# Cross-attention with prompt tokens: the bulk loads issued from GpSimd instead of SyncE

## The chip, the cores and the metric

The kernel runs on one core of a Trainium2 chip. A core has TensorE (PE) for matmuls, VectorE (DVE), ScalarE (ACT), GpSimd (POOL) and SyncE (SP), each with an instruction queue of its own that is worked off in order, and 16 DMA engines that move data between device memory and the on-chip memory. A transfer is started by an instruction in the queue of one of these engines; the engine that starts it need not be the one that uses the data. The metric is the device time of one execution, in microseconds (us). Before the change it is 423.75 us, the median of three runs from 422.22 to 429.26.

## What is computed

Eight batches of 112 rows of x (320 channels) attend to 375 context rows of 512 numbers each, in 20 heads of 16 channels. The last 4 context rows are prompt tokens with weights of their own. Cut to what matters:

```
q   = heads(x @ W_q)
k_t = heads(text @ W_k);  v_t = heads(text @ W_v)          # 371 rows
probs_t  = softmax(q k_t^T * scale)
text_out = probs_t v_t
k_ip = heads(ip @ W_k_ip); v_ip = heads(ip @ W_v_ip)       # 4 rows
qsem  = l2norm(probs_t text);  sem = qsem l2norm(ip)^T
probs_ip = softmax(q k_ip^T * scale + 0.5 * sem) * mask
out = (text_out + probs_ip v_ip) @ W_out + b_out + x
```

All in fp32.

## The kernel before, in words

**Tiling and order.** A batch is worked off in 5 groups of 4 heads (`steps`, line 1101: 40 pairs of batch and group). PE's four row groups of 32 take one head each. Heavy work of a group is `multiplied` (line 768): the transposed probabilities of 4 heads, in 12 blocks of 32 context rows, times a matrix `u`. `u` holds for each block of context rows the Gram matrix of the context (from which the length of qsem comes without qsem itself), the products with the prompt tokens, a column of ones, and 16 columns with the values of the head. The Gram part is made once for each batch (`gram`, line 516, `doubled`, line 502) and brought to all four row groups by DMAs (`gram_to_groups`, line 549). The 16 value columns differ from group to group: `placed` (line 681) copies them on POOL from `vr` into `u`, in three chunks of four blocks (the copies of line 688). A chunk's copy for the next group has to wait until PE has read that chunk for the present group, and PE cannot begin the chunk in the next group before the copy is done. `u` has two buffers, for even and odd batches.

**What comes before a group.** PE makes the scores (line 719), DVE their maximum (line 742), ACT the exponentials (line 745), a DMA of SP deals the probabilities out to the row groups (`sent`, line 754, tile xg), DVE transposes them (line 762). Between the groups stands the work for the next batches: context transposed (line 437), keys (line 577), values (line 611), Gram matrix (line 535), queries (lines 363 to 386, from x in blocks, tile xr_sb, which DVE transposes on line 365). After a batch `finish` (line 844) and `prompt_sums_and_projection` (line 968) work its output out; POOL multiplies the prompt values there (lines 970 to 978), and PE needs the result for line 983.

**Loads.** Context rows of batch 2 and later come by `load_ctx_blocks` (line 150): four DMAs of 352 rows of 512 bytes and four of 19 rows, after a memset of the last block on POOL (line 156), into tile ct, which has two buffers. x comes by `load_x_blocks` (four DMAs of 28 partitions, line 127, into the two places of xr_sb) and once more whole by `load_x` (line 1212, x_sb) for the residual. The prompts' values go to device memory (line 334) and come back once for each batch as `vip` (line 644) or, for the last two batches, by way of `vipx` and `bd` (lines 651 and 663). The second copy of W_q (rows in another order, lines 121 and 122), the prompts' weights (line 137, wkip_sb and wvip_sb), W_out (lines 133 and 134), mask and bias (lines 1217 and 1218) come while the first batch is under way. All of these are issued by SP, whose queue also carries xg, u (line 553), vd and vr (the values by way of device memory, lines 627 and 636) and the output. The first loads (lines 178 to 193: context of batches 0 and 1, W_v, x of batch 0, W_q, W_k) are SP's too.

**What sets the order.** The program is recorded by a framework that plans the order of each engine's queue. `tc.manual_schedule` keeps the written order: in the prologue (line 96, closed on line 1209) for all engines, for the main loop for PE, SP, DVE (line 93) and ACT (line 1245). POOL is among them only from line 1324 on, for the last batch. Elsewhere the planner places POOL's instructions, and may put one far ahead of where it is written if what it depends on is there and its buffer is free. For each queue that issues DMAs the framework has eight semaphores, used in turn: a DMA also waits until the one eight before it has landed.

```
    def placed(b, g, chunks=range(NT)):
        s = st[b]
        for c in chunks:
            v = region(b, c)[:, :, UV - c * P :]
            ...
            nc.gpsimd.tensor_copy(v, dealt(b, c, s["vr"][:, c * QN : (c + 1) * QN, g, :]))
...
    engines = {mybir.EngineType.PE, mybir.EngineType.SP, mybir.EngineType.DVE}
    ctx.enter_context(tc.manual_schedule(engines=engines))
```

Of the kernel before, what the change touches and what calls it, by code (L numbers as in the profile page):

```python
# [20 lines left out]
def kernel(  # L21
# [14 lines left out]
    nc = tc.nc  # L36
    P = 128
    B, S, C = x.shape
# [46 lines left out]
    def bank(name, spare=False):  # L85
# [13 lines left out]
    x_sb = const.tile([S, B, C], F32, tag="x_sb", name="x_sb")  # L99

    xr_sb = const.tile([P, 2, QN, C // QN + 4], F32, tag="xr_sb", name="xr_sb")
    wq_sb = const.tile([P, NC, CP], F32, tag="wq_sb", name="wq_sb")
# [4 lines left out]
    wkip_sb, wvip_sb = (  # L107
        work.tile([P, NIP, H, D], F32, tag="vipb", name=name).rearrange("p e h d -> p e (h d)")
        for name in ("wkip_sb", "wvip_sb")
    )  # L110
    wo_sb = const.tile([P, NC, C], F32, tag="wo_sb", name="wo_sb")
    ip_sb = const.tile([N, E], F32, tag="ip_sb", name="ip_sb")
    sm_sb = const.tile([S, 1], F32, tag="sm_sb", name="sm_sb")
    bias_sb = const.tile([S, C], F32, tag="bias_sb", name="bias_sb")
# [3 lines left out]
    def load_pairs(eng, t, w):  # L118

        w = w.rearrange("(p c) f -> p c f", c=5)  # L120
        eng.dma_start(t[0::2, :, :C], w[:, :3, :])
        eng.dma_start(t[1::2, :2, :C], w[:, 3:, :])

    def load_x_blocks(b, j):

        for a in range(QN):
            nc.sync.dma_start(
                xr_sb[a * RG : a * RG + S // QN, j, :, :XB],
                x[b, :, a * XB : (a + 1) * XB].rearrange("(q i) f -> i q f", q=QN),
            )  # L130

    def load_channels(eng, t, w):
        eng.dma_start(t[:, :FULL, :C], w[: FULL * P, :].rearrange("(i p) f -> p i f", p=P))
        eng.dma_start(t[:REST, FULL, :C], w[FULL * P :, :])

    def load_embed(eng, t, w):
        eng.dma_start(t[:, :, :C], w.rearrange("(p e) f -> p e f", e=NE))
# [12 lines left out]
    def load_ctx_blocks(b, blocks=range(QN)):  # L150

        full = TT // RG
        if b not in loaded:
            ct = io.tile([P, NT, E], F32, tag="ct", name=f"ct_{b}")
            v = ct.rearrange("p c e -> p (c e)").rearrange("p (j f) -> p j f", f=P)
            nc.gpsimd.memset(v[:, full, :], 0.0)
            loaded[b] = v
        v = loaded[b]
        for a in blocks:
            nc.sync.dma_start(  # L160
                v[a * RG : (a + 1) * RG, :full, :],
                ehs[b, : full * RG, a * P : (a + 1) * P].rearrange("(j i) f -> i j f", i=RG),
            )
        for a in blocks:
            nc.sync.dma_start(
                v[a * RG : a * RG + TT - full * RG, full, :],
                ehs[b, full * RG : TT, a * P : (a + 1) * P],
            )

    def load_ctx(b):  # L170
        if b >= LEAD:
            load_ctx_blocks(b)
            return loaded[b]
        ct = io.tile([P, NT, E], F32, tag="ct", name=f"ct_{b}")
        for c in range(NT):
            rows = min(P, T - c * P)
            some = rows - rows % 16
            nc.sync.dma_start(ct[:some, c, :], ehs[b, c * P : c * P + some, :])
            if some < rows:
                nc.sync.dma_start(ct[some:rows, c, :], ehs[b, c * P + some : c * P + rows, :])  # L180
        return ct
# [71 lines left out]
    vipx = dram.tile([2, H, NIP, C], F32, tag="vipx", name="vipx", bufs=1)  # L253
# [387 lines left out]
    def prompt_values(b):  # L641

        st[b]["vip"] = work.tile([P, NIP, H, D], F32, tag="vipb", name=f"vip_{b}")[:S]
        nc.sync.dma_start(
            st[b]["vip"].rearrange("p n h d -> p (n h d)"),
            vipd[b * NIP : (b + 1) * NIP, :].rearrange("n c -> (n c)").partition_broadcast(S),
        )

    def prompt_values_by_head():

        nc.sync.dma_start(
            vipx,
            vipd[N - 2 * NIP :, :]
            .rearrange("(b n) c -> b n c", n=NIP)
            .unsqueeze(1)
            .to_broadcast([2, H, NIP, C]),
        )

    def load_prompt_values_by_head():
        t = io.tile([P, NT, E], F32, tag="ct", name="bd")  # L660
        st[B - 1]["xb"] = t[:S, 2, :C]
        bd = t[:HN, :2, :CP]
        nc.sync.dma_start(bd[:, :, :C], vipx.rearrange("b h n c -> (h n) b c"))
        return bd

    def own_channels(bd):
# [14 lines left out]
# [5 lines that stand above are left out]
            if b > 0 and c > 0:  # L686
                v = v.rearrange("p (i j) d -> p i j d", i=2)
            nc.gpsimd.tensor_copy(v, dealt(b, c, s["vr"][:, c * QN : (c + 1) * QN, g, :]))  # L688
# [49 lines left out]
    def probabilities(b, g, a, hold=False):  # L738
        s = st[b]
        ps = s.pop(("sc", g, a))  # L740
        nmx = small.tile([S, 1], F32, tag="nmx", name=f"nmx_{b}_{g}_{a}", bufs=4)
        nc.vector.tensor_reduce(nmx, ps[:S, :TT], AX.X, ALU.max, negate=True)  # L742
        if ("p", g) not in s:
            s["p", g] = home(b, g)
        nc.scalar.activation(s["p", g][:, a, :], ps[:S, :TT], AF.Exp, bias=nmx)  # L745
        if b > 0:
            nc.scalar.copy(s["ipl"][:, groups[g][a], :], ps[:S, TT:T])  # L747
        if not hold:
            sent(b, g, a)
# [442 lines left out]
    drain(transposed_context(1))  # L1192
    run(("q", 0), None)
    nc.gpsimd.memset(wq_sb[:, FULL, :], 0.0)
    load_pairs(nc.sync, wq_sb, w_q)
    load_x_blocks(1, 0)
    run(("k", 0), None)
    for a in range(GROUP):
        scores(0, 1, a, early=True)
        probabilities(0, 1, a)  # L1200
    load_embed(nc.sync, wkip_sb, w_k_ip)
    load_embed(nc.sync, wvip_sb, w_v_ip)
    placed(0, 0)
    transposed(0, 0)
    run(("k", 0), None)
# [3 lines left out]
    prologue.close()  # L1209

    def load_x(b0, b1):
        nc.sync.dma_start(x_sb[:, b0:b1, :], x[b0:b1].rearrange("b s c -> s b c"))

    def load_rest(n):

        if n == 3:
            nc.sync.dma_start(sm_sb, smask.unsqueeze(1))
            nc.sync.dma_start(bias_sb, b_out.partition_broadcast(S))
        elif n == NG + 1:
            load_channels(nc.sync, wo_sb, w_out)  # L1220
        if g == NG - 1:
            load_x(b, b + 1 if b < B - 2 else B)

# [22 lines left out]
    for n, (b, g) in enumerate(steps[:-NG]):  # L1246
# [5 lines left out]
        for j, _ in enumerate(multiplied(b, g)):  # L1252
            if j == 0:
                for c, a in now if late else ():
                    scores(*c, a)
                    probabilities(*c, a)
                for c, a in more:
                    scores(*c, a, ps=bank(f"ps_s_{c[0]}_{c[1]}_{a}"))
                    probabilities(*c, a, hold=True)
            if j == 6:  # L1260
                for c, a in then:
                    scores(*c, a)
            if j == 2:
                if g == 0:
                    gram_banks(b + 1)
                transposed(*steps[n + 1])
                for c, a in more:
                    sent(*c, a)
                if 1 <= g <= 3:
                    gram_to_groups(b + 1, {1: (0,), 2: (1,), 3: (3,)}[g], parts=halves[g == 2])  # L1270
                for c, i in x_loads.get((b, g), ())[: int(n > 0)]:
                    load_x_blocks(c, i)

                if g in (1, 2) and b > 0:
                    run(("f", b - 1), None)
# [14 lines left out]
        if g == 0 and b > 1:  # L1290
            run(("f", b - 2), None)
        load_rest(n)
        if n == 0:
            load_next(2)
        if g in ctx_blocks and b < B - 3:
            load_ctx_blocks(b + 3, ctx_blocks[g])
        for c, i in x_loads.get((b, g), ())[1:]:
            load_x_blocks(c, i)
# [10 lines left out]
        if (b, g) == (B - 2, 0):  # L1309
            prompt_values_by_head()  # L1310
        if (b, g) == (B - 2, 1):
            bd = load_prompt_values_by_head()
        if g == 0 and b > 0:
            prompt_values(b - 1)
# [15 lines left out]
    b = B - 1  # L1330
# [6 lines left out]
    for g in range(NG):  # L1337
# [28 lines left out]
        n = (3, 3, 2, 1)[g]  # L1366
# [90 lines left out]
```

## Time and profile before

| | us |
|---|---|
| median of three runs | 423.75 |
| the profiled execution | 426.04 |
| its span, first to last instruction | 424.3 |
| PE busy | 415.8 |
| DVE busy | 331.5 |
| ACT busy | 185.5 |
| POOL busy | 111.2 |

The profile is of one execution. Busy time is the time in which an engine has an instruction under way; PE's matmuls are pipelined and their ends are modelled, so a busy PE is not PE at its peak. Issues of DMAs and waits are not counted as busy. A row of a timeline has the start, the time taken, engine, line, operation, output and input with shapes, a count, and in brackets the idle time before it and what ended that. A row of the busy times by stage has the stretch, its length, the busy time of PE, PE's weight loads, DVE, ACT and POOL with their instruction counts, the clock granted to TensorE (1.00 is full), the share of the DMA engines and GB/s. Over the span the granted clock is 0.999, and the DMA engines move 155 GB/s on the mean, nearly all of it from SP's queue.

### The profile page before, as it was taken

What the parts mean: (1) busy time and instruction counts of PE and PEld (TensorE: products, weight loads), DVE (VectorE), ACT (ScalarE), POOL (GpSimd) and SP (SyncE); (2) the same over time, 40 slices, a digit from 0 to 9 for tenths busy, and PEclk for the clock granted to TensorE, in tenths of its full rate; (3) what the DMA queues carried; (4) which work ended last, traced back from release to release, by engine and by line L of the source; (5) the groups of instructions that cost most, each with busy time, mean ns of one, the idle gap of its engine ahead of it and who ended that gap; (6) DMA issues with size and microseconds to landing.
All of it is one profiled execution on the core that took longest, in us unless ns stands there. A gap on an engine that the chain in (4) does not pass through costs nothing.

```text
span 424.3 us, 14021 instructions
## 1 busy us (share of the span) xinstructions
PE 415.8 (98%) x5500; PEld 327.3 (77%) x5500; DVE 331.5 (78%) x693; ACT 185.5 (44%) x647; POOL 111.2 (26%) x277
## 2 busy tenths in 40 slices
PE   8999999999998999999999999999999999999995
PEld 8867767878776977779778887788778887787993
DVE  5037668869896987889789987987898986888873
ACT  2344332335333463334533463333634363446773
POOL 6411100011160120602133220602124120515550
PEclk9999999999999999999999999999999999999999
DMA  8676846565766565666656556655555556465200
GB/s 256 184 191 198 187 122 181 155 174 152 192 157 169 141 170 154 158 175 175 169 142 167 144 158 164 159 145 158 167 151 151 134 162 181 135 167 166 66 2 29
DMA packets 61687, 65.84 MB, mean 155 GB/s; under 512 B 22072, under 2 KB 55648, under 8 KB 61622
## 3 DMA queue, kind: packets, MB, share of 16 engines
q1 hardware_dynamic: 60990, 63.98, 56.5%
q8 instruction: 44, 0.72, 0.8%
q10 hardware_dynamic: 632, 0.96, 0.7%
q14 instruction: 21, 0.17, 0.1%
HBM read 20.23 MB, written 5.32 MB: 60 GB/s over the span
## 4 chain that ended last, share of the span: by engine, by line
PE 83%; DVE 4%; ACT 3%; DMA 3%; issue 3%; SPq 2%; POOL 0%; DVEq 0%; POOLq 0%
PE ps_qd L781 34%; PE ps_v L611 14%; PE ps_k L577 10%; PE ps_s L719 9%; PE ps_g L535 7%; DMA xg<-p 2%; PE ps_q L377 2%; PE ps_o L995 2%; PE ps_g L491 1%; DVE xgT L762 1%; DVE nmx L742 1%; ACT shared L820 1%; SPq L553 1%; PE ps_w L467 1%; SPq L636 1%
## 5 line engine op out<-in xcount | busy, mean ns | idle before, releaser
L781 PE MATMUL ps_qd<-u,xgT 32*112 32x360 f32 (+11 forms) x3840 | 219.5, 351 | 1.2 <-POOL u L688 1.2
L781 PEld LDWEIGHTS ps_qd<-u,xgT 32*112 32x112 f32 x3840 | 189.1, 172 | 27.0 <-POOL u L688 2.4
L762 DVE STREAM_TRANSPOSE xgT<-xg 128x1536 f32<-128x1536 f32 (+1 forms) x45 | 119.7, 2680 | 13.9 <-DMA xg<-p 9.4
L745 ACT ACTIVATE p<-ps_s,nmx 112x371 f32<-112x371 f32 x156 | 84.9, 586 | 61.5 <-DVE nmx L742 49.3
L742 DVE TENSOR_REDUCE nmx<-ps_s 112x1 f32<-112x371 f32 x160 | 76.9, 526 | 28.3 <-PE ps_s L719 27.3
L827 DVE CUSTOM_DVE_ANT_0 junk<-ps_qd,p 112x371 f32<-112x371 f32 x146 | 79.2, 543 | 17.9 <-PE ps_qd L781 1.5
L719 PE MATMUL ps_s<-kT,qm 32*112 32x375 f32 (+1 forms) x320 | 66.7, 497 | 0.0
L688 POOL COPY u<-vr 128x64 f32<-128x64 f32 x120 | 25.7, 236 | 152.5 <-PE ps_qd L781 90.2
L611 PE MATMUL ps_v<-wv_sb,ctxT 128*128 128x384 f32 (+1 forms) x192 | 63.0, 477 | 0.0
L611 PEld LDWEIGHTS ps_v<-wv_sb,ctxT 128*128 128x128 f32 x192 | 35.7, 190 | 20.9
L794 ACT COPY pvs<-ps_qd 112x21 f32<-112x21 f32 x151 | 16.2, 189 | 74.8 <-PE ps_qd L781 74.5
L577 PE MATMUL ps_k<-ctxT,wk_sb 128*128 128x371 f32 x136 | 46.9, 488 | 0.2 <-DVE ctxT L458 0.2
L577 PEld LDWEIGHTS ps_k<-ctxT,wk_sb 128*128 128x128 f32 x136 | 24.4, 189 | 14.0 <-issue 0.5
L719 PEld LDWEIGHTS ps_s<-kT,qm 32*112 32x112 f32 x320 | 23.7, 170 | 12.6 <-issue 10.9
L535 PE MATMUL ps_g<-ctxT 128*32 128x375 f32 (+11 forms) x672 | 30.4, 333 | 0.0
L535 PEld LDWEIGHTS ps_g<-ctxT 128*32 128x32 f32 x672 | 27.7, 110 | 2.0
L618 ACT COPY vext<-ps_v 128x384 f32<-128x384 f32 (+1 forms) x24 | 11.2, 465 | 40.0 <-PE ps_v L611 39.5
L747 ACT COPY ipl<-ps_s 112x4 f32<-112x4 f32 x140 | 24.3, 174 | 0.0
L386 DVE TENSOR_SCALAR qm<-ps_q,emask 128x224 f32<-128x224 f32 (+1 forms) x25 | 9.0, 394 | 17.3 <-PE ps_q L377 17.2
L970 POOL TENSOR_TENSOR wv<-vip,w 112x1280 f32<-112x1280 f32 x6 | 14.8, 2464 | 27.7 <-DVE w L910 27.7
L437 DVE STREAM_TRANSPOSE ctxT<-ct 128x512 f32<-128x512 f32 x18 | 20.0, 1110 | 0.0
L508 POOL TENSOR_TENSOR ug<-ug,half 128x128 f32<-128x128 f32 (+1 forms) x24 | 10.4, 447 | 30.6 <-ACT ug L507 30.6
(174 smaller groups left out, 320.7 us busy)
## 6 DMA issues: line engine op xcount, KB each, us to landing
xg<-p SPq DMA_DIRECT2D x156, 162.3 KB
u<-ug SPq DMA_DIRECT2D x124, 99.0 KB
ct<-in_ctx_dram SPq DMA_DIRECT2D x24, 176.0 KB
vr<-vd SPq DMA_DIRECT2D x32, 120.0 KB
vip<-vipd SPq DMA_DIRECT2D x6, 560.0 KB
vd<-vext SPq DMA_DIRECT2D x7, 320.0 KB
vd<-vext SPq DMA_DIRECT2D x7, 160.0 KB
out_dram<-ob SPq DMA_DIRECT2D x8, 140.0 KB
```

Source lines behind the costliest of these rows:

```text
L437: nc.vector.transpose(ctxT[:, :, c * P : (c + 1) * P].rearrange("p e (j i) -> p j e i", i=RG), ct[:, some, :].rearrange("p j (k e) -> p j ...
L535: nc.tensor.matmul(ps[c][q * RG : (q + 1) * RG, j * RG - c * P : T - c * P], ctxT[:, e, j * RG : (j + 1) * RG], ctxT[:, e, j * RG : T], st ...
L577: nc.tensor.matmul(ps[:, :TT], wk_sb[:, e, i * P : (i + 1) * P], s["ctxT"][:, e, :TT], start=(e == 0), stop=(e == NE - 1),)
L611: nc.tensor.matmul(ps[:, :w], ctxT[:, e, c * P : (c + 1) * P], wv_sb[:, e, :w], start=(e == 0), stop=(e == NE - 1),)
L688: nc.gpsimd.tensor_copy(v, dealt(b, c, s["vr"][:, c * QN : (c + 1) * QN, g, :]))
L719: nc.tensor.matmul(ps[:S, :w], qm[a * RG : (a + 1) * RG, i, r, j * S : (j + 1) * S], s["kT"][a * RG : (a + 1) * RG, i, :w], start=True, st ...
L742: nc.vector.tensor_reduce(nmx, ps[:S, :TT], AX.X, ALU.max, negate=True)
L745: nc.scalar.activation(s["p", g][:, a, :], ps[:S, :TT], AF.Exp, bias=nmx)
L747: nc.scalar.copy(s["ipl"][:, groups[g][a], :], ps[:S, TT:T])
L762: nc.vector.transpose(xT[:, j : j + n].rearrange("p j (k q) -> p q j k", q=QN), xg[:, :, j * RG : (j + n) * RG].rearrange("p q (j k) -> p ...
L781: nc.tensor.matmul(banks[a][:S, j * RG : UW], xT[a * RG : (a + 1) * RG, j, :S], region(b, c)[a * RG : (a + 1) * RG, q, j * RG - c * P :], ...
L827: nc.vector.tensor_tensor_reduce(out=junk, in0=ps[:S, :TT], in1=s["p", g][:, a, :], scale=1.0, scalar=0.0, op0=ALU.mult, op1=ALU.add, accu ...
```

## The change

Every load that SP issued after the first ones is issued by GpSimd, in its own transfer queue; data, shapes, buffers and the written place stay. What stays on SP: the loads of lines 178 to 193, xg, u, vd, vr, vipd and the output. ACT's few DMAs stay as well.

```diff
 def load_x_blocks(b, j):
-            nc.sync.dma_start(
+            nc.gpsimd.dma_start(
                 xr_sb[a * RG : a * RG + S // QN, j, :, :XB],
 def load_ctx_blocks(b, blocks=range(QN)):
-            nc.sync.dma_start(
+            nc.gpsimd.dma_start(
                 v[a * RG : (a + 1) * RG, :full, :],
...
-            nc.sync.dma_start(
+            nc.gpsimd.dma_start(
                 v[a * RG : a * RG + TT - full * RG, full, :],
 def prompt_values(b):
-        nc.sync.dma_start(
+        nc.gpsimd.dma_start(
             st[b]["vip"].rearrange("p n h d -> p (n h d)"),
 def prompt_values_by_head():
-        nc.sync.dma_start(
+        nc.gpsimd.dma_start(
             vipx,
 def load_prompt_values_by_head():
-        nc.sync.dma_start(bd[:, :, :C], vipx.rearrange("b h n c -> (h n) b c"))
+        nc.gpsimd.dma_start(bd[:, :, :C], vipx.rearrange("b h n c -> (h n) b c"))
...
-    load_pairs(nc.sync, wq_sb, w_q)
+    load_pairs(nc.gpsimd, wq_sb, w_q)
...
-    load_embed(nc.sync, wkip_sb, w_k_ip)
-    load_embed(nc.sync, wvip_sb, w_v_ip)
+    load_embed(nc.gpsimd, wkip_sb, w_k_ip)
+    load_embed(nc.gpsimd, wvip_sb, w_v_ip)
 def load_x(b0, b1):
-        nc.sync.dma_start(x_sb[:, b0:b1, :], x[b0:b1].rearrange("b s c -> s b c"))
+        nc.gpsimd.dma_start(x_sb[:, b0:b1, :], x[b0:b1].rearrange("b s c -> s b c"))
 def load_rest(n):
-            nc.sync.dma_start(sm_sb, smask.unsqueeze(1))
-            nc.sync.dma_start(bias_sb, b_out.partition_broadcast(S))
+            nc.gpsimd.dma_start(sm_sb, smask.unsqueeze(1))
+            nc.gpsimd.dma_start(bias_sb, b_out.partition_broadcast(S))
...
-            load_channels(nc.sync, wo_sb, w_out)
+            load_channels(nc.gpsimd, wo_sb, w_out)
```

## The prediction

> **What bounds the kernel now.** I read the page first (busy shares, chain, groups), then PE's busy time by stage, then POOL's timeline beside PE's, because POOL is the engine that gets the new work.
>
> ```profile
> span 424.3 us, 14021 instructions
> PE 415.8 (98%) x5500; PEld 327.3 (77%) x5500; DVE 331.5 (78%) x693; ACT 185.5 (44%) x647; POOL 111.2 (26%) x277
> ...
> PE 83%; DVE 4%; ACT 3%; DMA 3%; issue 3%; SPq 2%; POOL 0%; DVEq 0%; POOLq 0%
> ...
> L781 PE MATMUL ps_qd<-u,xgT 32*112 32x360 f32 (+11 forms) x3840 | 219.5, 351 | 1.2 <-POOL u L688 1.2
> ...
> L688 POOL COPY u<-vr 128x64 f32<-128x64 f32 x120 | 25.7, 236 | 152.5 <-PE ps_qd L781 90.2
> ```
>
> PE is busy 98% of the span and is 83% of the chain, SP's queue 2%. POOL is idle three quarters of the time, and what it does for PE is small: 120 copies of 0.24 us (L688), which put the next group's values into u. They are just in time: they wait for PE to leave a region of u (90.2 us of waits) and PE has lost 1.2 us to them. A POOL that comes late stops PE.
>
> ```profile
> 80.00:90.00 10.00, 9.32 (x124) 7.96 (x120) 8.58 (x17) 3.34 (x14) 0.99 (x5) 1.00 0.58 147
> ...
> 130.00:140.00 10.00, 8.67 (x123) 6.83 (x116) 6.79 (x13) 3.17 (x13) 0.59 (x3) 1.00 0.61 155
> ```
>
> By stage (second column: PE busy of 10 us) PE stands still for 0.68 and 1.33 us in the two worst stages before the end. There is almost nothing for a better transfer queue to win.
>
> **The change part by part.** It takes 99 DMA issues out of SP's queue: 28 of xr_sb, 24 of 352 rows and 24 of 19 rows of ct, 7 of x_sb, 6 of vip, 4 of the second wq and the prompts' weights, 2 of wo, sm, bias, vipx, bd. The loads before line 195 and the first wq stay on SP. The bytes are the same. On POOL the scopes of fixed order do not hold the main loop's work, so the planner places the issues among POOL's copies; the order in which the changed program's instructions stand shows where, and PE's, DVE's and ACT's orders are unchanged. Each issue also waits for the landing of the eighth one before it, as SP's did.
>
> SP's gain: 99 issues of some 0.3 to 0.5 us. SP's queue is 2% of the chain, so I credit only the 1.33 us stop, which has time to vanish when PE comes later; the 0.68 us one is dealt with under (b).
>
> The price of an issue on POOL, called d, is in no row, since nothing is issued from POOL before. Bounds:
>
> ```profile
> L160 SPq DMA_DIRECT2D ct<-in_ctx_dram x24: 408/523/1283, 46.0 to 288.4; - x24
> L165 SPq DMA_DIRECT2D ct<-in_ctx_dram x24: 224/319/363, 48.7 to 289.2; - x24
> ...
> 139.55 0.53 SPq L1212 DMA_DIRECT2D x_sb<-in_x_dram  x1
> ...
> 142.35 0.87 POOL L841 TENSOR_TENSOR xb<-x_sb,bias_sb 112x320 f32<-112x320 f32 x1 [4.32 <-DMA x_sb<-in_x_dram]
> ```
>
> Lower end: SP spends 0.32 us (19 rows) to 0.52 us (352 rows). Upper end: POOL held until the data has landed, 142.35 - 139.55 = 2.8 us. I take d = 1.0 us, twice SP's price, nearer the low end because the flight does not occupy the issuer. The Trainium skill, page "DMA: Bandwidth & Descriptors", gives about 1 us of emission overhead for GpSimd ("Latency and other measured facts"), by which the sum would be the one below; its section "Anatomy of one DMA — SWDGE (gpsimd) path" calls descriptor generation small and puts the dispatch at about 50 ns, by which the sum would be rival B. No run here shows either yet.
>
> (a) The start. 33 issues stand ahead of the first L688: sm even ahead of the identity that PE's first matmul needs; bias, wo and x_sb; all of ct_2 between the first ug products and the spreading of wq and wk; eight of xr_sb, five of x_sb, the second wq, both prompts' weights.
>
> ```profile
> 0.00:29.20 29.20, 27.51 (x158) 22.99 (x159) 10.00 (x24) 10.47 (x24) 11.73 (x50) 1.00 0.72 213
> ...
> 0.81 0.20 POOL masks.py:197 MEMSET ident<- 128x128 f32 x1 [0.29 <-POOLq L1439]
> ...
> 37.03 0.58 PE L781 MATMUL ps_qd<-u,xgT 32*112 32x392 f32 x2
> ...
> 40.32 0.24 POOL L688 COPY u<-vr 128x64 f32<-128x64 f32 x1 [4.82 <-PE ps_qd L781]
> ```
>
> POOL's work to that L688 is 11.73 us (sixth column), plus 0.87 for L841, which now stands ahead of it, plus 0.8 before POOL begins: 13.4 + 33d = 46.4 at d = 1. The copy ends 0.24 later, at 46.6; PE wants it at 37.03. Stop: 9.6 us. The small delays ahead of it (the identity, ug) disappear inside, as POOL then never rests. The cover is used up at d = 0.71.
>
> The second row gives a length needed below: PE leaves the first chunk of u 3.3 us after a group begins (40.32 - 37.03), so the second chunk's copy has that much more time.
>
> (b) Between batch 0 and 1. All eight issues of ct_4 stand between the memset L156 and the copy for the next batch.
>
> ```profile
> 81.66 0.20 POOL L156 MEMSET ct<- 128x128 f32 x1
> 88.94 0.58 POOL L688 COPY u<-vr 128x64 f32<-128x64 f32 x3 [7.07 <-DMA vipd<-ipkv]
> ...
> 87.19 1.35 PE L719 MATMUL ps_s<-kT,qm 32*112 32x375 f32 x4
> 89.23 3.89 PE L781 MATMUL ps_qd<-u,xgT 32*112 32x392 f32 x54 [0.68 <-POOL u L688]
> ```
>
> 81.86 + 8d + 0.24 = 90.1 against PE free at 88.54: 1.6 us where 0.68 was; net 0.9.
>
> (c) Batches 1, 2, 3, last group. Between POOL's work for the previous batch's output (L970 to L978) and the copy for group 4 stand the ct loads of batch b+4; in batches 1 and 3 four of xr_sb too. So 9, 8 and 9 issues precede the first chunk's copy, and in batches 1 and 3 four more (the rest of ct, vip) the second's.
>
> ```profile
> 127.07 0.59 POOL L688 COPY u<-vr 128x64 f32<-128x64 f32 x3
> ...
> 129.34 0.58 PE L781 MATMUL ps_qd<-u,xgT 32*112 32x392 f32 x2
> ...
> 176.71 0.59 POOL L688 COPY u<-vr 128x64 f32<-128x64 f32 x3
> ...
> 180.06 0.58 PE L781 MATMUL ps_qd<-u,xgT 32*112 32x392 f32 x2
> ...
> 226.19 0.59 POOL L688 COPY u<-vr 128x64 f32<-128x64 f32 x3
> ...
> 228.02 0.58 PE L781 MATMUL ps_qd<-u,xgT 32*112 32x392 f32 x2
> ```
>
> Batch 1: first chunk 127.31 + 9d - 129.34 = 9d - 2.0; second 127.5 + 13d - 132.6 = 13d - 5.1, the larger: 7.9 us. Batch 2: 176.95 + 8d - 180.06 = 4.9. Batch 3: 226.6 + 13d - 231.3 = 8.3. The work behind these copies (ACT's and DVE's for the next groups) is PE's successor and moves with it.
>
> The xr_sb issues also wait there, for DVE to be done with the buffer, and the copies stand behind that wait:
>
> ```profile
> 121.56 0.72 DVE L365 STREAM_TRANSPOSE xT<-xr_sb 128x128 f32<-128x128 f32 x3
> ```
>
> In batch 1 it is met at 122.3, before POOL comes to them (after 127); I put it at nothing.
>
> (d) Batch 4: only bd and vip, two issues.
>
> ```profile
> 272.54 0.86 POOL L978 TENSOR_TENSOR attn<-attn,wv 112x320 f32<-112x320 f32 x1
> 273.63 0.59 POOL L688 COPY u<-vr 128x64 f32<-128x64 f32 x3
> ...
> 275.58 0.45 PE L983 MATMUL ps_a<-ident,attn 112*128 112x112 f32 x3
> 277.13 0.58 PE L781 MATMUL ps_qd<-u,xgT 32*112 32x392 f32 x2
> ```
>
> L978 ends at 273.40, PE wants it at 275.58: 2.2 us cover 2d. Nothing, and nothing after. If d were over 1.1 the cover would be gone, at 2d - 2.2.
>
> (e) What a stopped PE does to its clock.
>
> ```profile
> 3.55 1.13 PE L450 MATMUL ps_c<-ident,ct 128*128 128x128 f32 x4
> ...
> 25.66 1.70 PE L450 MATMUL ps_c<-ident,ct 128*128 128x128 f32 x12
> ...
> 420.90:424.30 3.40, 0.00 (x0) 0.00 (x0) 0.49 (x1) 0.00 (x0) 0.00 (x0) 0.91 0.14 42
> ```
>
> The same transposes take 0.28 us each early and 0.14 later: half speed for the first 5 us or so. The clock's mean in the 3.4 us after PE's last matmul is 0.91, so it fell again some 2.8 us into the quiet if it falls to half. Four of the stops are longer than that; each then costs up to half of 5 us, or nothing; I take 2, so 8 us. The Trainium skill, page "TensorE: Matmul & The Clock Gate", Part 1, says that an idle window of about 3.4 us halves the clock and a busy one restores it. By that rule it would be 1.7 a stop, 6.8 in all; the trace agrees on the half.
>
> **Sum** at d = 1: 9.6 + 0.9 + 7.9 + 4.9 + 8.3 = 31.6, + 8 for the clock, - 1.3 for SP: 38 us. The profiled execution took 426.04 us around its span of 424.3, so it would become 464; against the median of the runs, 423.75, which is 2.3 less, 462.
>
> **The rivals.** B, not slower: the issue is cheap. Up to d = 0.18 no copy is late anywhere (9d - 1.6 = 0 in batch 3 decides), and only SP's relief is left, the two stops of 2.0 us: 422. For it: SP's 0.32 us is near; against: a copy of 64 elements takes POOL 0.24. At d = 0.5 the last groups lose 2.5, 0.9 and 2.9: 6.3 - 1.3, giving 429, still within 2%.
>
> C, the landing holds POOL: with d = 2.8 the same formulas give 9.6 + 33 x 1.8 = 69.0, 15.3, 31.3, 19.3, 31.7 and 3.4 in batch 4, 170 + 8 - 1.3: 600. The wait for the eighth landing before makes a mild form of it: it binds when landings take over 8d. Against: at d = 1 eight issues last 8 us and the landing above took under 3.
>
> D, the clock stays up: 462 - 8 = 454.
>
> **How the numbers follow.** The forecast with d between 0.75 and 1.5 (D inside): at 0.75, 1.4 + 0 + 4.75 + 2.9 + 5.15 + 3 x 2 - 2.0 is 18, giving 442; at 1.5, 26.1 + 4.9 + 14.4 + 8.9 + 14.8 + 0.8 + 8 - 1.3 is 77, giving 500. Chance 0.62. Between 0.5 and 0.75 (429 to 442): 0.12. B, at or under 429: 0.12, of which 0.02 for a gain that I do not see. C and all over 500: 0.14, half of it under 515. The range 430 to 515 leaves out 0.12 and 0.07. Within 2% (415 to 432; about what a measurement of this kernel can tell from no change) lie 0.10 of B and 0.02 of the next case: 0.12. Slower by more 0.86, faster by more 0.02.
>
> **What would show it.** Right: idle PE ahead of L781 that ends on POOL u L688 in the tens of us, at about 37 and at the last groups of batches 1, 2, 3, none after batch 4; lower granted clock behind these stops; first L688 at about 46. Wrong: the first L688 still near 29 and no such waits (d is small); stops that end on a DMA into ct, xr_sb or vip (transfers late, not POOL); POOL's queue idle ahead of its issues (landings bind).

## The result and the profile after

The changed kernel takes 453.98 us in the median of 6 runs (452.98 to 455.81), the kernel before 423.68 in 6 runs beside it: a ratio of 1.0717, with a 95% interval of 1.0665 to 1.0768. The forecast was 462, range 430 to 515. Executions more than 1.5% above the fastest of the same kernel stand outside the ratios here and below. The profiled execution took 453.84 us around a span of 451.0, which is 26.7 longer than the span of before. That is the sum to be explained.

The page of the changed kernel, with the rows that answer to those of before (busy time and mean behind the bar, then idle time and what ended it):

```profile
span 451.0 us, 14036 instructions
...
PE 426.3 (95%) x5500; PEld 331.0 (73%) x5500; DVE 330.9 (73%) x693; ACT 185.2 (41%) x647; POOL 168.6 (37%) x376
...
q0 software_dynamic: 5328, 12.84, 11.9%
...
PE 69%; POOL 9%; DVE 7%; DMA 7%; issue 3%; ACT 3%; SPq 1%; DVEq 0%; POOLq 0%; ACTq 0%
...
L781 PE MATMUL ps_qd<-u,xgT 32*112 32x168 f32 (+11 forms) x3840 | 226.4, 360 | 13.4 <-issue 7.0
...
L762 DVE STREAM_TRANSPOSE xgT<-xg 128x1536 f32<-128x1536 f32 (+1 forms) x45 | 119.3, 2670 | 29.6 <-DMA xg<-p 27.6
...
L688 POOL COPY u<-vr 128x64 f32<-128x64 f32 x120 | 26.1, 237 | 142.1 <-PE ps_qd L781 99.5
```

PE's share of the chain fell from 83 to 69%, POOL's rose from 0 to 9 and the DMAs' from 3 to 7: there are two new limits, not one. POOL has 168.6 - 111.2 = 57.4 us more to do, for 99 issues: 0.58 us each. On POOL an issue shows as busy time.

The rows of the tile ct give the price by size (min/median/max in ns):

```profile
L160 POOL DMA_DIRECT2D ct<-in_ctx_dram x24: 625/651/688, 12.0 to 253.0; - x24
L165 POOL DMA_DIRECT2D ct<-in_ctx_dram x24: 512/530/559, 19.2 to 254.1; - x24
...
DMA to landing us min/median/max: 2.8/5.9/9.6
```

352 rows cost 0.65 us, 19 rows 0.53. So d is 0.58, not 1.0. The landings take up to 9.6 us.

Where the 26.7 us arise is read by setting the first L781 of each group against the same one of before; the growth from group to group is

| stretch | us later | what stands there |
|---|---|---|
| start to first L781 | 9.5 | PE waits for L762, L762 for xg |
| first group | 1.5 | half clock |
| end of batch 0 | -2.9 | one of before's stops is gone (0.68), and the 1.35 us of L719 that stood alone ahead of it now run beside L781; the rest was not followed |
| batch 1, groups 0 to 2 | 7.4 | L762 waits for xg, half clock behind it |
| up to the last group of batch 1 | 3.2 | L688 behind issues |
| that group | 0.1 | half clock, less before's other stop (1.33) |
| up to the last group of batch 2 | 1.4 | L688 behind issues |
| up to the last group of batch 3 | 4.2 | L688 behind issues |
| that group | 1.7 | half clock |
| the rest | 0.6 | mostly the last group of batch 2; not followed |

**The start.** The timeline of POOL, DVE and PE in the changed kernel (start, time taken, engine, line; in brackets the idle time before and what ended it):

```profile
37.37 0.57 POOL L137 DMA_DIRECT2D wkip_sb<-in_L_xattn_W_k_ip_dram  x1 [2.07 <-DMA ct<-in_ctx_dram]
...
38.77 0.58 POOL L688 COPY u<-vr 128x64 f32<-128x64 f32 x3
...
43.57 2.88 DVE L762 STREAM_TRANSPOSE xgT<-xg 128x1536 f32<-128x1536 f32 x1 [8.15 <-DMA xg<-p]
...
46.55 1.01 PE L781 MATMUL ps_qd<-u,xgT 32*112 32x392 f32 x4 [6.97 <-issue]
```

POOL's first copies are there at 38.77, 7.8 us ahead of PE. What PE waits for is DVE's transpose: it ends at 46.45, and had stood idle 8.15 us for xg, which SP sends. In the kernel before this transpose was ready for a first L781 at 37.03. The profile names no releaser for PE here ("issue"), and its chain runs over POOL's work on wq_sb, which ends at 43.07; the ground for this reading is that L781 follows the end of L762 by 0.10 us. The first row also shows an issue standing 2.07 us for a landing of ct.

The same place by stages (PE busy is the second column, the granted clock the third from the end, then the DMA engines' share):

```profile
40.00:50.00 10.00, 3.45 (x25) 2.14 (x29) 3.67 (x3) 1.42 (x4) 4.50 (x12) 0.66 1.01 259
110.00:120.00 10.00, 8.66 (x89) 7.30 (x93) 8.76 (x19) 5.89 (x14) 2.18 (x6) 0.66 0.31 83
...
148.00:151.40 3.40, 3.35 (x28) 2.06 (x32) 2.89 (x1) 0.00 (x0) 3.40 (x8) 0.60 1.22 222
...
250.00:260.00 10.00, 6.90 (x100) 5.25 (x100) 4.66 (x6) 1.15 (x4) 5.70 (x14) 0.83 1.11 196
```

Around 46 us the DMA engines are full (share 1.01), at 259 GB/s. Around or behind each stop of 2.3 us and more the granted clock is down, to 0.60 to 0.83 in these stretches.

**Batch 1, first groups.** The same views for the place where the second loss arises:

```profile
91.78 0.66 POOL L160 DMA_DIRECT2D ct<-in_ctx_dram  x1
...
96.95 1.09 POOL L644 DMA_DIRECT2D vip<-vipd  x2
...
99.10 0.63 POOL L651 DMA_DIRECT2D vipx<-vipd  x1 [1.05 <-DMA ct<-in_ctx_dram]
...
107.40 2.89 DVE L762 STREAM_TRANSPOSE xgT<-xg 128x1536 f32<-128x1536 f32 x1 [7.59 <-DMA xg<-p]
111.34 1.49 PE L719 MATMUL ps_s<-kT,qm 32*112 32x375 f32 x2 [3.68 <-ACT ipl L747]
```

Within 8 us the planner lets go all of ct_4, vip_0, vip_1 and vipx, about 2 MB (176 and 9.5 KB four times each, 560 KB twice, 200 KB). The chain of waits has the xg that SP sends meanwhile as one piece:

```profile
97.37 9.91 DMA xg<-p
```

In the kernel before the longest pieces of this kind in the chain are 3.12 us. Here one of the 162 KB transfers of xg takes three times as long, and the transpose, the scores and PE wait for it.

**The last groups** of batches 1, 2 and 3, in the timeline:

```profile
144.69 2.40 POOL L127 DMA_DIRECT2D xr_sb<-in_x_dram  x4
147.08 0.67 POOL L160 DMA_DIRECT2D ct<-in_ctx_dram  x1
147.75 0.25 POOL L688 COPY u<-vr 128x64 f32<-128x64 f32 x1
...
148.05 5.45 PE L781 MATMUL ps_qd<-u,xgT 32*112 32x392 f32 x56 [2.33 <-POOL u L688]
...
200.25 3.03 PE L781 MATMUL ps_qd<-u,xgT 32*112 32x392 f32 x40 [0.53 <-POOL u L688]
...
253.10 4.50 PE L781 MATMUL ps_qd<-u,xgT 32*112 32x392 f32 x40 [3.34 <-POOL u L688]
...
301.45 0.58 POOL L688 COPY u<-vr 128x64 f32<-128x64 f32 x3
```

Here it is as the forecast said: the copy comes right behind a row of issues, PE 0.3 us behind the copy. At the end of batch 4 (last row) nothing stops.

### The profile page after: what moved, and what is told of

Same layout as the page of the kernel before. It is cut to its first block, busy times and chain, and to the rows that moved or that the text cites. A ratio compares the mean times of both kernels' runs of the same rounds, so it can differ in the third digit from the quotient of the medians.

```text
span 451.0 us, 14036 instructions
## 1 busy us (share of the span) xinstructions
PE 426.3 (95%) x5500; PEld 331.0 (73%) x5500; DVE 330.9 (73%) x693; ACT 185.2 (41%) x647; POOL 168.6 (37%) x376
## 3 DMA queue, kind: packets, MB, share of 16 engines
q0 software_dynamic: 5328, 12.84, 11.9%
## 4 chain that ended last, share of the span: by engine, by line
PE 69%; POOL 9%; DVE 7%; DMA 7%; issue 3%; ACT 3%; SPq 1%; DVEq 0%; POOLq 0%; ACTq 0%
PE ps_qd L781 33%; PE ps_v L611 9%; PE ps_s L719 7%; PE ps_g L535 6%; PE ps_k L577 5%; DMA u<-ug 3%; PE ps_o L995 2%; PE ps_q L377 2%; DMA xg<-p 2%; DVE xgT L762 2%; DVE junk L827 2%; DMA wq_sb<-in_L_xattn_W_q_dram 2%; POOL wv L970 2%; POOL ct L160 2%; PE ps_g L491 1%
## 5 line engine op out<-in xcount | busy, mean ns | idle before, releaser
L781 PE MATMUL ps_qd<-u,xgT 32*112 32x168 f32 (+11 forms) x3840 | 226.4, 360 | 13.4 <-issue 7.0
L781 PEld LDWEIGHTS ps_qd<-u,xgT 32*112 32x112 f32 x3840 | 190.8, 176 | 46.3 <-issue 11.5
L762 DVE STREAM_TRANSPOSE xgT<-xg 128x1536 f32<-128x1536 f32 (+1 forms) x45 | 119.3, 2670 | 29.6 <-DMA xg<-p 27.6
L688 POOL COPY u<-vr 128x64 f32<-128x64 f32 x120 | 26.1, 237 | 142.1 <-PE ps_qd L781 99.5
L719 PE MATMUL ps_s<-kT,qm 32*112 32x375 f32 (+1 forms) x320 | 67.0, 501 | 3.7 <-ACT ipl L747 3.7
L719 PEld LDWEIGHTS ps_s<-kT,qm 32*112 32x112 f32 x320 | 23.9, 171 | 16.2 <-issue 10.8
L535 PE MATMUL ps_g<-ctxT 128*32 128x375 f32 (+11 forms) x672 | 30.4, 333 | 0.0
L535 PEld LDWEIGHTS ps_g<-ctxT 128*32 128x32 f32 x672 | 27.7, 110 | 2.0
L618 ACT COPY vext<-ps_v 128x384 f32<-128x384 f32 (+1 forms) x24 | 11.1, 465 | 41.2 <-PE ps_v L611 37.6
L508 POOL TENSOR_TENSOR ug<-ug,half 128x128 f32<-128x128 f32 (+1 forms) x24 | 10.4, 448 | 29.6 <-ACT ug L507 29.6
```

The lines of the kernel that those rows point to most:

```text
L535: nc.tensor.matmul(ps[c][q * RG : (q + 1) * RG, j * RG - c * P : T - c * P], ctxT[:, e, j * RG : (j + 1) * RG], ctxT[:, e, j * RG : T], st ...
L719: nc.tensor.matmul(ps[:S, :w], qm[a * RG : (a + 1) * RG, i, r, j * S : (j + 1) * S], s["kT"][a * RG : (a + 1) * RG, i, :w], start=True, st ...
L762: nc.vector.transpose(xT[:, j : j + n].rearrange("p j (k q) -> p q j k", q=QN), xg[:, :, j * RG : (j + n) * RG].rearrange("p q (j k) -> p ...
L781: nc.tensor.matmul(banks[a][:S, j * RG : UW], xT[a * RG : (a + 1) * RG, j, :S], region(b, c)[a * RG : (a + 1) * RG, q, j * RG - c * P :], ...
```

## The experiments

Three theories were put to the test. "Issue time": an issue keeps POOL 0.6 us from a copy that PE waits for. "Place" (crowding): on POOL the planner lets loads go early and together, and their bytes slow SP's xg. "Second queue": bulk loads slow xg because they are on another queue than SP's, wherever they stand. All medians stand beside runs of the kernel before on the same chip.

### The whole in parts

Four kernels each take one part of the change. The edit of the second, as an example (load_x_blocks has the same one):

```diff
         for a in blocks:
-            nc.sync.dma_start(
+            nc.gpsimd.dma_start(
                 v[a * RG : (a + 1) * RG, :full, :],
```

x_sb, W_out, mask and bias alone:

> Only x_sb, W_out, mask and bias on POOL (11 issues), which the planner puts into the first 29 us; the rest with SP. Crowding theory: 1.98 MB more in the first 30 us than before, a first stop of 2 to 4 us, total 426 to 429 us. Issue theory: 11 issues of 0.6 us ahead of the first copy, 13.4 + 6.6 = 20 us against 37: no stop there, and none later: 424 us.

427.17 us, ratio 1.0012 [0.9974, 1.0049]: no difference that can be measured.

ct and xr_sb alone, 76 issues:

> Only the loads made once for each batch, ct and xr_sb (76 issues), on POOL. Issue theory: the stops ahead of the last groups of batches 1, 2 and 3 as in the changed kernel (3.2, 1.4 and 4.2 us, with the half clock behind them 10 to 12 in all), 434 to 437 us. Crowding theory: these and a part of the first stop, since ct of batch 2 comes 30 us earlier, 437 to 441 us.

439.92 us, ratio 1.0320 [1.0248, 1.0391]. Its timeline has the stops of the last groups again, here batch 3:

```profile
239.07 0.26 POOL L688 COPY u<-vr 128x64 f32<-128x64 f32 x1
...
239.39 5.45 PE L781 MATMUL ps_qd<-u,xgT 32*112 32x392 f32 x56 [2.43 <-POOL u L688]
```

vip, vipx and bd alone, 8 issues:

> Only the prompts' values (vip, vipx, bd: 8 issues) on POOL. In the changed kernel two vip loads and vipx, 1.3 MB, are issued together at 97 to 100 us, where the transposes of batch 1's first groups wait 7.6 us for xg. Crowding theory: 2 to 5 us of that stop, 426 to 430 us. Issue theory: 3 issues ahead of a copy with room: 424 us.

441.14 us, ratio 1.0340 [1.0268, 1.0411]: 14.7 us for 8 issues of 0.6, far more than expected. No copy of POOL is late in this kernel. Its timeline:

```profile
87.64 1.26 POOL L644 DMA_DIRECT2D vip<-vipd  x2
88.88 0.65 POOL L651 DMA_DIRECT2D vipx<-vipd  x1
...
95.65 3.02 DVE L762 STREAM_TRANSPOSE xgT<-xg 128x1536 f32<-128x1536 f32 x1 [6.59 <-DMA xg<-p]
...
99.71 1.09 PE L719 MATMUL ps_s<-kT,qm 32*112 32x375 f32 x3 [2.62 <-ACT ipl L747]
```

Three loads, 1.3 MB, stand ahead of an xg, and DVE waits 6.59 us. So 8 loads let go at the wrong time cost as much as all 76 of ct and xr_sb.

The second wq and the prompts' weights alone:

> Only the second W_q and the prompts' weights (4 issues, 1.68 MB) on POOL. They stand ahead of the first copy in the written order too, so they come about 5 us earlier than with SP. Crowding theory: a first stop of 1 to 3 us, 424 to 427 us. Issue theory: none, 424 us.

427.93 us, ratio 1.0043 [1.0009, 1.0077]. The parts come to 0.7 + 13.4 + 14.7 + 1.5 = 30.3 us, the whole to 453.98 - 423.68 = 30.3. The equality is luck, for the parts do not add up. The next kernel, all but the constants, lost 448.38 - 426.29 = 22.1 us where its parts come to 29.6; the constants, which cost nothing measurable alone, make the other 8 in company. And a loss at the start is in part won back: with the weights alone the second group begins 5.6 us late, batch 2 only 1.5. Neither these weights nor ct and xr_sb make the start's 9.5 us alone: with them the first L781 comes 3.9 and 2.4 us late.

### All but the constants

The changed kernel with x_sb, W_out, mask and bias back on SP:

> The changed kernel with the loads that are needed late (x_sb, W_out, mask, bias: 11 issues, 1.98 MB, all put into the first 29 us by the planner) left on SP. Crowding theory: a third or more of the bytes are gone from the first 46 us, the first stop falls from 9.5 us to 3 to 5 us, total 446 to 449 us. Issue theory: the first copy was at 38.8 us already and was not what PE waited for, the last groups of batches 1 to 3 are as they were: no change from 454 us.

448.38 us, ratio 1.0539 [1.0447, 1.0630], as crowding had it. The first L781 comes at 40.04 instead of 46.55, again 0.10 us behind its transpose, but the next transpose waits instead:

```profile
37.04 2.90 DVE L762 STREAM_TRANSPOSE xgT<-xg 128x1536 f32<-128x1536 f32 x1 [3.47 <-DMA xg<-p]
...
40.04 5.30 PE L781 MATMUL ps_qd<-u,xgT 32*112 32x392 f32 x56 [2.30 <-issue]
...
48.84 3.09 DVE L762 STREAM_TRANSPOSE xgT<-xg 128x1536 f32<-128x1536 f32 x1 [8.12 <-DMA xg<-p]
```

With the constants gone the first stop shrinks and the crowding strikes a group later: the weights and ct_2 are still let go there.

### Issues without bytes

The kernel before, POOL held to the written order, with 13 loads of 16x16 numbers issued from POOL ahead of the last group's copies in batches 1, 2, 3:

```diff
-    engines = {mybir.EngineType.PE, mybir.EngineType.SP, mybir.EngineType.DVE}
+    engines = {..., mybir.EngineType.Pool}
...
+        if g == 3 and 1 <= b <= 3:
+            for k in range(13):
+                nc.gpsimd.dma_start(scr[:, b - 1, k, :], x[0, :16, 16 * k : 16 * k + 16])
         placed(*steps[n + 1])
```

Its control has the first edit alone:

> Control: the kernel before, with POOL too held to the written order in the main loop; all loads still issued by SP. POOL's copies keep their places ahead of each group, so all theories expect the time of before, 424 us within 1%. If the planner's order of POOL is worth something by itself, it shows here: over 428 us.

428.47 us, ratio 1.0052 [1.0006, 1.0099]: the written order alone costs 2.2 us, in stops of 0.69 at L535, which waits for the copy L520. With the loads:

> The control (SP issues every load, POOL in written order) plus 13 extra loads of 16 x 64 bytes issued by POOL just ahead of the copy for the last group of batches 1, 2 and 3: issue time with hardly a byte moved. Issue theory, at 0.55 us each 7.2 us ahead of the copies with 2.0, 3.1 and 1.6 us of room: stops of about 5.1, 4.1 and 5.5 us plus up to 2 us each at half clock, 15 to 20 us over the control. Crowding and queue theory: no bytes, no change, 424 us.

449.44 us, ratio 1.0565 [1.0501, 1.0629], 21 us over the control. Line numbers in this kernel are one higher (L689 is the copy, L782 the matmul). Its timeline in batch 1:

```profile
126.34 6.40 POOL L1292 DMA_DIRECT2D scr<-in_x_dram  x13
132.73 0.58 POOL L689 COPY u<-vr 128x64 f32<-128x64 f32 x3
133.03 1.66 PE L782 MATMUL ps_qd<-u,xgT 32*112 32x392 f32 x8 [4.36 <-POOL u L689]
```

13 issues take 6.40 us, 0.49 each, and PE stands for 4.36 us (3.08 and 4.22 in batches 2 and 3; expected 5.1, 4.1 and 5.5 by a dearer issue). They move 1 KB each, so no bytes are to blame: an issue ahead of a copy that PE needs costs its time. The stops come to 11.7 of the 21 us; the clock granted behind them is down to 0.66 and 0.83. By the first L781 of each group these three places hold 18.7 us (0.7 in the control): 14.3 up to the group, 4.4 within it.

### All loads in the written order

The changed kernel with POOL in the written order, so that no load goes earlier than SP issued it:

> The changed kernel (99 issues on POOL) with POOL held to the written order, so that no load is issued earlier than it was by SP. Crowding theory (the planner puts loads far ahead and in bunches, which fills the DMA engines while the probabilities xg are on their way): no stop behind xg at the start or in batch 1, about 424 to 428 us. Issue theory (0.6 us of POOL per issue, 9 to 13 of them ahead of the copies of the last groups): the issues now stand spread over the groups, 8 to 12 at most ahead of a copy that has over 5 us of room, so at most 3 us over the control. Queue theory (a second queue takes its share from SP's transfers wherever its loads stand): still 440 us or more.

451.51 us, ratio 1.0619 [1.0545, 1.0692]: hardly better. What crowding foretold did come: the first L781 is 2.5 us late instead of 9.5, and the chain has no landing of xg before batch 6 (7.79 and 5.86 us there). But my expectation had overlooked the copy L520, which the Gram matrix of the next batch waits for. In the written order it stands behind the step's loads:

```profile
45.44 2.58 POOL L160 DMA_DIRECT2D ct<-in_ctx_dram  x4
...
48.01 2.05 POOL L165 DMA_DIRECT2D ct<-in_ctx_dram  x4
50.05 2.42 POOL L127 DMA_DIRECT2D xr_sb<-in_x_dram  x4
52.46 0.21 POOL L520 COPY ctxT<-ipnT 128x16 f32<-128x16 f32 x1
...
52.72 2.08 PE L535 MATMUL ps_g<-ctxT 128*32 128x375 f32 x12 [7.76 <-POOL ctxT L520]
```

Twelve issues, 7.05 us, and PE stands 7.76. Over the kernel L535 waits 20.1 us for L520, by the view of that line; in the control it is 4.8. That is 15.3 of the 451.51 - 428.47 = 23.0 us.

### Written order, the loads last in each step

The same, with each step's other POOL work written ahead of its loads:

```diff
+        between(b, g)
         load_rest(n)
...
         if g == 0 and b > 0:
             prompt_values(b - 1)
-        between(b, g)
```

> All loads on GpSimd in written order as in the kernel at 451.5, but each step's other POOL work (the copy L520 that the gram waits for, the copies into kT, the finishing of a batch) is written ahead of the step's loads, so that no copy that PE needs soon stands behind an issue. Theory 'issue time' (an issue of 0.5 to 0.7 us on POOL ahead of a copy that PE waits for): the stops of 7.8 and 4.0 us and the extra 0.85 us per batch go, the 1.8 us before the first L781 stays: control 428.5 + 1.8 + some clock = 430 to 434. Rival 'second queue' (bulk transfers on POOL's queue slow SP's small ones wherever they stand): it stays at 445 or more, with DVE L762 waiting for xg. Anything between says that both have a share.

443.28 us, ratio 1.0419 [1.0329, 1.0509]: between the two forecasts. L535's wait for L520 is down to 4.7 us, the control's, so there the issue's price is gone. Its profiled execution had a granted clock of 0.95 over the span, so the rest cannot be placed in it. Hence the next one, in which L520 costs the same 4.7 us at a clock of 0.994, without the start's loads (weights, x_sb, mask, bias on SP):

> Only the loads of the loop (ct, xr_sb, vip, vipx, bd: 84 of the 99 issues) on GpSimd, in written order, with each step's other POOL work ahead of its loads; weights, x_sb, mask and bias back on SP, so that the start is as before. In the planner's order these loads lost 13.5 us (ct, xr_sb alone) and 14.5 us (vip, vipx, bd alone). Theory 'issue time and place' (an issue costs PE time only ahead of a copy that PE waits for, a load only where it is let loose early or in a bunch): no such copy stands behind an issue any more: control 428.5, up to 433 with an xr_sb or vip that crowds one xg; L535's wait for L520 stays at the control's 0.7 us a batch. Rival 'second queue': 440 or more whatever the place, with DVE L762 waiting for xg at several groups. Between 433 and 440: both have a share.

436.94 us, ratio 1.0299 [1.0253, 1.0345]. In the planner's order these 84 loads and the four of the weights cost 22.1 us together (the kernel without the constants), the weights alone 1.5. Here the 84 cost 11.9, of which 2.2 are the control's. So some 9 to 10 us were order alone: what the planner set ahead of the copies, and what it let go early. Of the 9.7 left over the control, 4.6 arise in one place, batch 6:

```profile
352.65 0.69 POOL L651 DMA_DIRECT2D vipx<-vipd  x1
353.34 0.53 POOL L644 DMA_DIRECT2D vip<-vipd  x1
...
356.79 1.85 SPq L754 DMA_DIRECT2D xg<-p  x2
...
366.76 2.96 DVE L762 STREAM_TRANSPOSE xgT<-xg 128x1536 f32<-128x1536 f32 x1 [4.58 <-DMA xg<-p]
```

This xg takes from 357.77 to 366.57, 8.8 us, by the chain. In the kernel before the same two loads go out on SP's queue 6.6 us ahead of the same xg, which is issued at 349.51 and transposed at 355.22. The place differs by 3 us, the queue differs too. The next kernel bears on which of the two makes the 8.8 us.

### One vip a batch, at its old place

vip, vipx and bd on POOL as above, but in the written order:

> Only vip, vipx and bd on GpSimd, as in the kernel at 441.1, but in written order, so one vip a batch at the step where SP issued it. Theory 'place' (that kernel lost 14 us because the planner issued vip_0, vip_1 and vipx together, 1.3 MB at once, and each later vip early): the crowding goes, what is left is one issue ahead of L520 in each of six batches, 0.6 to 0.85 each: control 428.5 + 4 to 5 = 432 to 434, xg landings near those of before. Rival 'second queue': about 441 again, xg landings of 5 us and more behind a vip.

437.02 us, ratio 1.0283 [1.0210, 1.0356]: by time hardly to be told from the planner's order, and between the forecasts. But the loss has another ground. The view of L520 in this kernel:

```profile
who waited for it (us, times):
...
  PE ps_g L535: 11.1, 7
```

PE now waits 11.1 us for L520, 6.3 more than in the control, because a vip stands ahead of it in each batch; no landing of xg is left in the chain. That is 6.3 of the 437.02 - 428.47 = 8.5 us. On the old place a vip costs its issue, not its bytes. It holds in batch 6 too: vipx and vip go out on POOL's queue at 344.58 and 345.25, 13 us ahead of the xg that was so late with the loads last (here issued at 358.39), and DVE waits only 0.33 us for it. So POOL's queue alone does not make that stop; whether SP's would, at 3 us, was not tried.

### The same bunch on SP

The kernel before with vip_0, vip_1 and vipx issued together at the end of batch 0, on SP:

```diff
-        if (b, g) == (B - 2, 0):
+        if (b, g) == (0, NG - 1):
+            prompt_values(0)
+            prompt_values(1)
             prompt_values_by_head()
...
-        if g == 0 and b > 0:
+        if g == 0 and b > 2:
             prompt_values(b - 1)
```

> The kernel before, all on SP's queue, POOL free as before, but vip_0, vip_1 and vipx are issued together at the end of batch 0, about where the planner put them on POOL. Theory 'place': 1.3 MB at once ahead of xg and of u and vr costs one stop of 2 to 6 us in the first groups of batch 1, nothing later: 428 to 432. Rival 'second queue': the place alone is harmless, 425 to 428.

430.05 us, ratio 1.0107 [1.0003, 1.0211]: a small loss, by an interval that nearly reaches 1. By the first L781 of each group it falls 4.0 us behind the kernel before from the first group of batch 1 to the last; with the bunch on POOL the same stretch cost 5.3, each in one profiled execution. DVE stands for 5.26 us ahead of a transpose there, for 6.59 with the bunch on POOL. So at this place SP's own queue is little better: the place seems to do most of the harm, and the queue's share is not settled. What the kernel with vip on POOL lost beyond that goes with the later vips, which the planner issued as soon as L976 had read the buffer before. Here is that kernel's vip_4, ahead of SP's xg:

```profile
229.19 1.56 POOL L976 TENSOR_TENSOR wv<-wv 112x640 f32<-112x640 f32 x1
...
230.69 0.58 POOL L644 DMA_DIRECT2D vip<-vipd  x1
...
232.82 1.83 SPq L754 DMA_DIRECT2D xg<-p  x2
...
239.75 2.92 DVE L762 STREAM_TRANSPOSE xgT<-xg 128x1536 f32<-128x1536 f32 x1 [3.03 <-DMA xg<-p]
```

SP issues the corresponding load at 295.7 in the kernel before, 65 us later; here it stands 2 us ahead of an xg, and DVE waits 3.03 us for it.

## Why the forecast held, and where its steps failed

**The bound, and that a late POOL stops PE: right.** The issues without bytes show it by themselves.

**The price of an issue: the mis-sized term.** I took 1.0 us, from bounds of 0.32 and 2.8; it measured 0.58. The nearer end was the lower, SP's own price, and the issue of 352 rows on POOL (0.65) is only a quarter dearer than SP's 0.52.

**(c), the last groups: mechanism right, size off by d.** With 0.58 the prediction's formulas give 9d - 2.0 = 3.2, 8d - 3.1 = 1.5 and 9d - 1.6 = 3.6, 8.3 us together. Measured: 3.2, 1.4 and 4.2, 8.8. The forecast was 21.1. (d), nothing in batch 4: right.

**(a), the start: right number, wrong cause.** Forecast 9.6, measured 9.5. But the first L688 came at 38.77, not at 46, and by the prediction's own condition (a stop only from d = 0.71 on) POOL should have cost nothing. With just the 33 issues ahead of them POOL's copies came 6.2 us later than 13.4 + 33d, 3.3 of it in two waits for landings (1.20 for u, 2.07 for ct); had xg been on time, PE would still have stood 38.77 + 0.24 - 37.03 = 2.0 us for them. The step that failed is the one that counted only instructions: "the bytes are the same". They are, but 33 loads let go early filled the DMA engines (share 1.01), and xg came late. The kernel without the constants, whose first L781 comes 6.5 us earlier and whose next transpose then waits 8.12 us for xg, fits this, and so does the written order, where it comes 7.0 us earlier.

**(b), batch 0 to 1: wrong.** Net 0.9 was forecast. Of SP's two stops the 0.68 went here, which was forecast to grow, and the 1.33 in the last group of batch 1, as credited. But 7.4 came, with the half clock behind it, from crowding by ct_4, both vip and vipx. The prediction looked only at what stands ahead of L688 there; what is let go behind it, three loads of 1.3 MB and the ct_4 ahead of it, went with the harm.

**(e), the clock: about right.** Two us a stop were taken; the groups behind the stops lost 1.5 at the start, 0.1 + 1.33 = 1.4 in batch 1 and 1.7 in batch 3. Behind the stop of 3.68 in batch 1 the clock was 0.50 from 111.30 to 114.70 and 0.51 on to 118.00, by which an estimate is up to 3.3 us, inside the table's 7.4. Together that is about 8, as forecast. The Trainium skill, page "TensorE: Matmul & The Clock Gate", Part 1, halves the clock after an idle window of about 3.4 us. The trace agrees on the half and not on the length: the stop of 2.33 was enough for 0.60 in the 3.40 us behind it.

**The rivals.** B's price (0.5) was nearer than mine, its time (429) was not, for it has no crowding either. C, in its mild form, happened: with d at 0.58 eight issues last 4.6 us, half the landings of ct took 5.9 or more, and POOL stood 2.07 us for one. Had I known d, my formulas would have given 423.75 + 8.3 - 1.3 = 431 and a few us of clock; the over-priced issue and the missing term, crowding, nearly cancelled. The total of 454 against 462 says less for the forecast than it seems to.

**A rule on crowding.** The Trainium skill, page "DMA: Bandwidth & Descriptors", section "Queues, rings and completion order", has each DMA engine take turns between the queues that have work for it. By that rule a second queue's bulk load takes a share of every engine from xg at once; the 9.91 and 8.8 us of xg fit it, but the bunch on SP's single queue lost most of what the one on POOL's did (4.0 against 5.3), so this case shows the crowding and not the rule.

**Open:** the 5 us beside the stop in batch 6 with the loads last, what a second queue adds at a place that is bad on either, and how the start's 9.5 us divides among weights, ct and constants.

## What to carry to other kernels

Before moving a DMA issue to a compute engine, list the small instructions of that engine that the bound engine waits for, and count issues ahead of each at the price of an issue there; a planner that orders that queue may put them in front. Then count the bytes that the move lets go earlier or together, against the small transfers on the critical path: here 8 loads at the wrong time cost as much as 76 others with all their issues. Such losses do not add up part by part, so measure the parts in company too. A forecast whose total is right should still be held against its own signs, one by one.

## What was not expected of the hardware

An issue on POOL depends little on its size: 0.49 us for 16 rows of 64 bytes, 0.53 for 19 rows, 0.65 for 352. And SP's own issues can be held up: with vip on POOL one issue of xg on SP took 5.29 us, with the DMA engines full around it (share 1.05 from 92.20 to 97.50), where the longest of before was 1.56. Full engines alone do not do it: in the changed kernel, with a share of 1.08 from 28 to 46 us, no issue of xg took over 0.97. The line's own view in the kernel with vip on POOL (min/median/max in ns):

```profile
L754 SPq DMA_DIRECT2D xg<-p x156: 800/858/5287, 26.8 to 408.3; - x156
```
